# Row tiles of a selective scan: both directions' rows side by side in DRAM, the middle group's partitions interleaved, and the next tile's pieces in a new order

## The chip, the cores and the metric

The kernel runs on one core of one Trainium2 chip. The metric is the device time of one launch in microseconds (us), as the median of several runs. All engine times below come from one profiled execution of the program.

The engines are named as in the profile: PE is TensorE (matmuls; PEld its weight loads), DVE is VectorE, ACT is ScalarE, POOL is GpSimd and SP is the sync engine, which here does nothing but issue DMAs, in order, each after the semaphores that it needs.

## The reference

The input is x, of 2 images x 96 channels x 128 x 128 in fp32. The model is two blocks. The first mixes with a four-direction Mamba, the second with a 3x3 convolution, and each is followed by a small feed-forward net in emulated low precision. The change concerns the Mamba alone:

```python
x = x + L0_conv(_ln_c(x))          # norm over channels, then four scans
# L = 16384 positions; four orders: rows, rows reversed, columns, columns reversed
def _mamba(x, ...):                # D_INNER 192, D_STATE 16, DT_RANK 6, causal conv of 4 taps
    xc, z = split(x @ in_w.T)
    xc = silu(conv(xc) + conv_b)
    dt_raw, Bm, Cm = split(xc @ xproj_w.T)
    dt = softplus(dt_raw @ dt_w.T + dt_b)
    A = -exp(A_log)                # 192 x 16
    def step(h, t):                # h: 192 x 16
        h = exp(dt_t[:, :, None] * A) * h + dt_t[:, :, None] * B_t[:, None, :] * u_t[:, :, None]
        y = einsum('bds,bs->bd', h, C_t)
    y = (y + Dp * xc) * silu(z)
    return y @ outp_w.T
out = concat([y1, y2, y3, y4]) @ fuse_w.T + fuse_b
```

B_t and C_t are 16 numbers per position and direction, and every one of the 192 inner channels of that direction uses the same ones.

## The kernel before, in words

Each image (batch) passes three stages one after the other: `normalize`, `mamba`, and `ffn_and_conv`. `acc`, 96 x 16384 in SBUF, holds the running activations. `normalize` also writes the normalized input to DRAM twice, in row order (`xnr`) and in column order (`xnc`).

**Pairs, groups, tiles.** `mamba` takes the four directions as two pairs, (0, 2) forwards and (1, 3) reversed. The 2 x 192 = 384 inner channels of a pair make three groups of 128 partitions: group 0 is 128 channels of the first direction, group 2 is 128 channels of the second, and the middle group, 1, holds the last 64 of the first on partitions 0 to 63 and the first 64 of the second on 64 to 127. Time is cut into 32 tiles of T = 512 positions. So there are 64 tiles per batch (two pairs x 32), and 128 in all.

**Units.** A tile is worked through in 24 units, each one group and two of the 16 states: 8 units of group 0, 8 of group 1, 8 of group 2. The loop index k runs over all units of all tiles. For unit k:

- `decay` (L330, ACT): two exponentials give `da`, 128 x 2 x 512, in PSUM; three buffers.
- `b_part` (L324, POOL): the row tile of B times `dtu` (dt times u), in place.
- `scan` (L334, DVE): two scans of 512 positions, written over `da`.
- `behind` (one unit later): the product of `da` with the row tile of C (L409, DVE), the last column kept in `hst` (L410, ACT), and `sums` (L341, PE), which adds the two states' products into `y` by matmuls with the identity.
- At a group's first unit, `gated` (L349, DVE) multiplies the finished `y` of the previous group with the gate `sz`, and a matmul with `dmat` (L416, PE) begins a new `y`. `y` has a single PSUM bank.
- `project` and `collect` (L357 to L365) take a finished pair of groups through the output weights `gmat` into `acc`.

`decay` and `b_part` run two units ahead of the scan (`AHEAD = 2`).

**Row tiles.** B and C are wanted on all partitions, so the rows are written to DRAM once per tile and read back as broadcasts. `rows` (L251) projects xc to 64 rows (and the 12 of dt), `rows_out` (L258 to L261) copies them to SBUF and writes them to DRAM four times (`COPIES = 4`), side by side as `bcd[copy, B or C, 32 rows, T]`. A row tile (`row_tile`, L320) is 128 partitions x 4 states x 512, 1 MB: a quad of states for one group. Each partition reads 8 KB, and the partitions take the four copies in turn. For groups 0 and 2 that is one DMA. The middle group's two halves belong to different directions, so its row tile takes two DMAs of 64 partitions. `fetch` issues a B tile every other unit three quads ahead and a C tile two quads ahead; there are four buffers of B rows and three of C rows.

**The next tile's pieces.** Tile n + 1 is prepared while tile n is scanned. `prologue` lists its pieces as (step, where, function): at unit `step` of tile n, either before the scans (`where` 0) or at the end of the unit (1). All five queues are written in program order (`in_order`), so the list settles the order in each engine's queue:

```python
at = [(0, 0, load), (8, 1, partial(silu, "xc")), (14, 1, partial(silu, "sz"))]
at += [(12, 0, rows), (12, 1, rows_out)]
for g, k in enumerate((4, 5, 6)):
    at += [(k, 0, partial(conv, g)), (k, 1, partial(conv_out, g))]
for g, k in enumerate((7, 10, 11)):
    at += [(k, 0, partial(gate, g)), (k, 1, partial(gate_out, g))]
for g, k in enumerate((13, 18, 21)):
```

`conv` and `gate` are matmuls into `misc`, a single PSUM bank that all these pieces and `project` share (`inproj`, L207); `conv_out` (L233) and `gate_out` (L241) are ScalarE's copies out of it. In the middle group the two directions' matmuls write partitions 0 to 63 and 64 to 127. `silu` (L244, L245) is one activation over all three groups between two loads of an activation table. The last loop places dt's pieces per group: `dt_in` (a matmul, L268), `dt_exp` and `dt_ln` (three ScalarE operations each, L273 to L284), then four GpSimd operations (L287 to L297).

Of the kernel before, what the change touches and what calls it, by code (L numbers as in the profile page):

```python
# [10 lines left out]
F32 = mybir.dt.float32  # L11
# [3 lines left out]
AF = mybir.ActivationFunctionType  # L15
# [5 lines left out]
C = 96  # L21
W = 128
L = W * W
T = 512
NT = L // T
R = T // W
S = 16
RK = 6
DI = 192
HID = 384  # L30
PAIRS = ((0, 2), (1, 3))
NG = 3
COPIES = 4
B_AHEAD = 3
C_AHEAD = 2
AHEAD = 2
# [1 line left out]
BCO = 32  # L38
NBC = 4 * S
# [3 lines left out]
def tile_metaformer(ctx: ExitStack, tc: tile.TileContext, a: dict, out: bass.AP):  # L43
    nc = tc.nc
# [22 lines left out]
    convb = const("convb", (128, 2, NG))  # L67
    bcw = const("bcw", (128, 2, NG, BCO + NBC))
    dtw = const("dtw", (2 * RK, 2, NG * 128))
# [6 lines left out]
    dmat = cpool.tile([128, 2, NG, 128], F32, name="dmat")  # L76
    gmat = cpool.tile([128, 2, NG + 1, C], F32, name="gmat")
    inx = cpool.tile([C, 4, 4, DI], F32, name="inx")
    nc.vector.memset(gmat, 0.0)
    with tc.tile_pool(name="prep", bufs=1) as pp, tc.tile_pool(name="prep_ps", bufs=2, space=PSUM) as pps:  # L80
        alog = pp.tile([128, 2, NG, S], F32, name="alog")
        nc.sync.dma_start(alog, a["alog"])
        nc.scalar.activation(alog, alog, AF.Exp)
        nc.vector.tensor_scalar_mul(amat, alog, -1.0)

        dskip = pp.tile([128, 2, NG], F32, name="dskip")
        nc.sync.dma_start(dskip, a["dskip"])
        for pi in range(2):
            for g in range(NG):
                nc.vector.tensor_scalar_mul(dmat[:, pi, g, :], ident, dskip[:, pi, g : g + 1])  # L90

        inxw = pp.tile([C, 4, DI], F32, name="inxw")
        nc.sync.dma_start(inxw, a["inx"])
        taps = pp.tile([C, 4, 4, DI], F32, name="taps")
        nc.sync.dma_start(taps, a["taps"].broadcast_to((C, 4, 4, DI)))
        for d in range(4):
            nc.vector.tensor_tensor(inx[:, d], taps[:, d], inxw[:, d, None, :].broadcast_to((C, 4, DI)), ALU.mult)
        outw = pp.tile([C, 4, DI], F32, name="outw")
        nc.sync.dma_start(outw, a["outw"])
        fusew = pp.tile([C, 4, C], F32, name="fusew")  # L100
        nc.sync.dma_start(fusew, a["fusew"])
        for pi, (da, db) in enumerate(PAIRS):

            pieces = [
                (slice(0, 128), da, 0, 128),
                (slice(0, 64), da, 128, 192),
                (slice(64, 128), db, 0, 64),
                (slice(0, 128), db, 64, 192),
            ]
            for g, (rows, d, lo, hi) in enumerate(pieces):  # L110
                ps = pps.tile([128, C], F32, name="ps")
                nc.tensor.matmul(ps[rows, :], outw[:, d, lo:hi], fusew[:, d, :], start=True, stop=True)
                nc.vector.tensor_copy(gmat[rows, pi, g, :], ps[rows, :])

    def layernorm(x, eps, dst, wp, psp, bufs=2, **cast):

# [66 lines left out]
    def mamba(acc, xnr, xnc):  # L183

        with ExitStack() as st:
            pool = lambda n, bufs, **kw: st.enter_context(tc.tile_pool(name=n, bufs=bufs, **kw))
            io, one, two, gen = pool("io", 1), pool("one", 1), pool("two", 2), pool("gen", 4)
            ps_w, ps_y, ps_m = (pool(n, k, space=PSUM) for n, k in (("ps_w", 3), ("ps_y", 1), ("ps_m", 1)))
            rows_d = pool("rows_d", 3, space=DRAM)
# [20 lines left out]
            def prologue(pi, i, d):  # L210

                rev = pi == 1
                lo = L - (i + 1) * T if rev else i * T
                src = []
# [13 lines left out]
                    d["ps"] = inproj(pi, g, lambda dd, k, lo, hi: inx[:, dd, k, lo:hi], src, (0, 1, 2, 3))  # L228

                def conv_out(g):  # L230
                    if g == 0:
                        d["xc"] = two.tile([128, NG, T], F32, name="xc")
                    nc.scalar.activation(d["xc"][:, g, :], d["ps"], AF.Identity, bias=convb[:, pi, g : g + 1])  # L233

                def gate(g):
                    d["ps"] = inproj(pi, g, lambda dd, k, lo, hi: inz[:, dd, lo:hi], src, (3,))

                def gate_out(g):
                    if g == 0:
                        d["sz"] = two.tile([128, NG, T], F32, name="sz")  # L240
                    nc.scalar.copy(d["sz"][:, g, :], d["ps"])  # L241

                def silu(name):
                    nc.scalar.activation(d[name], d[name], AF.Silu)  # L244
# [8 lines left out]
                        )  # L253

                def rows_out():

                    d["rows"] = one.tile([BCO + NBC, T], F32, name="rows")
                    nc.scalar.copy(d["rows"], d["ps"][0 : BCO + NBC, :])  # L258
                    d["bcd"] = rows_d.tile([COPIES, 2, NBC // 2, T], F32, name="bcd")
                    for n in range(COPIES):  # L260
                        nc.sync.dma_start(d["bcd"][n].rearrange("k r t -> (k r) t"), d["rows"][BCO:, :])  # L261

# [35 lines left out]
                    d["dtu"].append(dtu)  # L298


                at = [(0, 0, load), (8, 1, partial(silu, "xc")), (14, 1, partial(silu, "sz"))]
                at += [(12, 0, rows), (12, 1, rows_out)]
                for g, k in enumerate((4, 5, 6)):
                    at += [(k, 0, partial(conv, g)), (k, 1, partial(conv_out, g))]
                for g, k in enumerate((7, 10, 11)):
                    at += [(k, 0, partial(gate, g)), (k, 1, partial(gate_out, g))]
                for g, k in enumerate((13, 18, 21)):
                    pieces = (0, 0, dt_in), (0, 1, dt_exp), (1, 1, dt_ln), (2, 0, dt_q), (3, 0, dt_log), (3, 0, dt_sum), (4, 0, dt_u)
                    at += [(k + m, where, partial(f, g)) for m, where, f in pieces]
                return sorted(at, key=lambda p: p[:2])  # L310

            def row_tile(d, g, s, k, ahead):

                t = gen.tile([128, 4, T], F32, name=f"row{k}", bufs=ahead + 1)
                for half in range(2) if g == 1 else (slice(None),):
                    rows = slice(half * 64, half * 64 + 64) if g == 1 else half
                    at = s + S * (half if g == 1 else g // 2)
                    n = (64 if g == 1 else 128) // COPIES
                    src = d["bcd"][None, :, k, at : at + 4, :].broadcast_to((n, COPIES, 4, T))
                    nc.sync.dma_start(t[rows], src)  # L320
                return t

            def b_part(d, g, b):
# [58 lines left out]
            for _, _, f in prologue(*steps[0], state[0]):  # L382
                f()
            bs, cs, das, hs = {}, {}, {}, {}

            def fetch(k, n, ahead, m):
                if k < total:
                    t = row_tile(state[k // nu], *units[k % nu], n, ahead)
                    m[k], m[k + 1] = t[:, 0:2, :], t[:, 2:4, :]
# [46 lines left out]
            for k in range(total + 6):  # L436
                n, u = divmod(k, nu)
# [128 lines left out]
def _layout(v):  # L566

    f = np.float32
    order = [d for pair in PAIRS for d in pair]
    rows = lambda w: w[order].reshape(2, NG, 128, -1).transpose(2, 0, 1, 3)  # L570
    xw = v["L0_conv_xproj_w"]
    bcw = np.zeros((2, 2 * DI, BCO + NBC), f)
    dtw = np.zeros((2 * RK, 2, 2 * DI), f)
    for pi, pair in enumerate(PAIRS):
        for k, d in enumerate(pair):
            at = slice(k * DI, (k + 1) * DI)
            for j in range(2):
                to = slice(BCO + (2 * j + k) * S, BCO + (2 * j + k + 1) * S)
                bcw[pi, at, to] = xw[d, RK + j * S : RK + (j + 1) * S].T
            bcw[pi, at, k * RK : (k + 1) * RK] = xw[d, :RK].T  # L580
            dtw[k * RK : (k + 1) * RK, pi, at] = v["L0_conv_dt_w"][d].T
    grouped = lambda w: w.reshape(2, NG, 128, -1).transpose(2, 0, 1, 3)
    out = {
        "x": v["x"].reshape(NB, C, L),
        "ident": np.eye(128, dtype=f),
        "inx": v["L0_conv_in_w"][:, :DI].transpose(2, 0, 1),
        "inz": v["L0_conv_in_w"][:, DI:].transpose(2, 0, 1),
        "taps": v["L0_conv_conv_w"].transpose(0, 2, 1)[None],
        "convb": rows(v["L0_conv_conv_b"])[..., 0],
        "bcw": grouped(bcw),  # L590
        "dtw": dtw,
        "dtb": rows(v["L0_conv_dt_b"])[..., 0],
        "alog": rows(v["L0_conv_A_log"]),
        "dskip": rows(v["L0_conv_Dp"])[..., 0],
        "outw": v["L0_conv_outp_w"].transpose(1, 0, 2),
        "fusew": v["L0_conv_fuse_w"].reshape(C, 4, C).transpose(2, 1, 0),
        "fuseb": v["L0_conv_fuse_b"].reshape(C, 1),
        "kw": v["L1_conv_kernel"].transpose(1, 2, 3, 0).reshape(C, 9, C),
    }
    for n in range(2):  # L600
        p = f"L{n}_ffn_"
        out[f"w1_{n}"] = v[p + "W1"].T
        out[f"b1_{n}"] = v[p + "b1"].reshape(3, 128).T
        out[f"w2_{n}"] = v[p + "W2"].T.reshape(3, 128, C).transpose(1, 0, 2)
        out[f"b2_{n}"] = v[p + "b2"].reshape(C, 1)
    return {k: np.ascontiguousarray(w) for k, w in out.items()}
# [16 lines left out]
```

## Time and profile before

| | before |
|---|---|
| time, median of 3 | 13002.14 us (12996.56 to 13002.71) |
| span of the profiled execution | 13002.5 us |
| first scan of batch 0, of batch 1 | 168 us, 6661 us |
| mean of a tile | 90.13 us |
| mean granted TensorE clock | 0.963 |
| DMA, whole span | 3400 MB, 262 GB/s |

The two scan stages, 128 tiles x 90.13 us, are 11,537 us of the 13,002. The time and the span are the same thing measured in two ways. A group of instructions in the profile is named by line, engine, operation and tiles (out<-in), and "<-" after a wait names the instruction whose end released it. The times inside a tile that are given below are from the tile that begins at 3138.95 us.

The DMAs that the change touches, with their size in KB and the median time from issue to landing in us:

```profile
row<-bcd SPq DMA_DIRECT2D x2048, 1024.0 KB, 7.5
row<-bcd SPq DMA_DIRECT2D x2048, 512.0 KB, 8.0
bcd<-rows SPq DMA_DIRECT2D x512, 128.0 KB, 9.8
```

### The profile page before, as it was taken

What the parts mean: (1) busy time and instruction counts of PE and PEld (TensorE: products, weight loads), DVE (VectorE), ACT (ScalarE), POOL (GpSimd) and SP (SyncE); (2) the same over time, 40 slices, a digit from 0 to 9 for tenths busy, and PEclk for the clock granted to TensorE, in tenths of its full rate; (3) what the DMA queues carried; (4) which work ended last, traced back from release to release, by engine and by line L of the source; (5) the groups of instructions that cost most, each with busy time, mean ns of one, the idle gap of its engine ahead of it and who ended that gap; (6) DMA issues with size and microseconds to landing.
All of it is one profiled execution on the core that took longest, in us unless ns stands there. A gap on an engine that the chain in (4) does not pass through costs nothing. (4 is left out here: it accounts for less than half of the span.)

```text
span 13002.5 us, 97992 instructions
## 1 busy us (share of the span) xinstructions
PE 10850.3 (83%) x24208; PEld 3987.1 (31%) x24208; DVE 11569.1 (89%) x10865; ACT 8560.0 (66%) x14738; POOL 9215.4 (71%) x4772
## 2 busy tenths in 40 slices
PE   6888888888888888888978888888888888888889
PEld 2323233333333333333323333332333333333233
DVE  5999999999999999995459999999999999999954
ACT  6666666666666666665566666666666666666655
POOL 4877778777787787772147778777787777877721
PEclk8999999999999999999989999999999999999999
DMA  7999999999999999992079999999999999999920
GB/s 226 287 294 282 298 288 285 295 283 298 288 285 295 283 295 289 285 295 68 13 226 285 298 283 292 290 285 298 285 291 291 284 298 286 290 294 281 296 61 13
DMA packets 545331, 3400.40 MB, mean 262 GB/s; under 512 B 81612, under 2 KB 82732, under 8 KB 146840
## 3 DMA queue, kind: packets, MB, share of 16 engines
q1 hardware_dynamic: 544760, 3394.12, 83.1%
q8 instruction: 195, 3.19, 0.1%
q14 instruction: 376, 3.08, 0.1%
HBM read 3288.94 MB, written 104.86 MB: 261 GB/s over the span
## 5 line engine op out<-in xcount | busy, mean ns | idle before, releaser
L324 POOL TENSOR_TENSOR row<-dtu,row 128x1024 f32<-128x1024 f32 x3072 | 7175.7, 2358 | 1739.3 <-DMA row<-bcd 1419.2
L334 DVE TENSOR_TENSOR_SCAN da<-da,hst,row 128x512 f32<-128x512 f32 x5952 | 7339.4, 1274 | 351.2 <-ACT da L330 194.6
L341 PE MATMUL y<-row,ident 128*128 128x512 f32 x12288 | 6120.1, 626 | 1113.3 <-DVE row L409 1098.9
L330 ACT ACTIVATE da<-dt,amat 128x512 f32<-128x512 f32 x6144 | 4249.4, 692 | 207.5 <-ACT hst L410 0.4
L341 PEld LDWEIGHTS y<-row,ident 128*128 128x128 f32 x12288 | 2288.9, 197 | 4779.4 <-DVE row L409 2292.3
L409 DVE TENSOR_TENSOR row<-da,row 128x1024 f32<-128x1024 f32 x3072 | 3705.9, 1206 | 19.6 <-DMA row<-bcd 18.8
L410 ACT COPY hst<-da 128x2 f32<-128x2 f32 x3072 | 484.0, 158 | 2235.5 <-DVE row L409 2233.3
L416 PE MATMUL y<-xc,dmat 128*128 128x512 f32 x768 | 526.1, 773 | 779.1 <-DVE sz L349 779.1
L287 POOL TENSOR_TENSOR q<-e,q 128x512 f32<-128x512 f32 x384 | 488.0, 1271 | 821.8 <-ACT hst L410 709.1
L233 ACT ACTIVATE xc<-misc,convb 128x512 f32<-128x512 f32 x384 | 264.2, 688 | 1117.5 <-PE misc L207 1117.5
L207 PE MATMUL misc<-xa,inx 96*128 96x512 f32 (+1 forms) x2048 | 932.4, 597 | 59.0 <-DMA xa<-xnr 57.2
L207 PE MATMUL misc<-xb,inx 96*64 96x512 f32 (+1 forms) x2048 | 928.1, 595 | 1.6 <-ACT xc L233 1.6
L531 POOL TENSOR_TENSOR acc<-acc,y 96x512 f32<-96x512 f32 x128 | 147.6, 1153 | 987.0 <-DVE y L530 987.0
L541 PE MATMUL pc<-pad,kw 96*96 96x512 f32 x1152 | 566.7, 593 | 0.0
L207 PEld LDWEIGHTS misc<-xa,inx 96*128 96x128 f32 (+1 forms) x2048 | 323.6, 163 | 625.5 <-issue 493.4
L293 POOL TENSOR_TENSOR dt<-dt,ln 128x512 f32<-128x512 f32 x384 | 486.9, 1268 | 30.1
L297 POOL TENSOR_TENSOR dtu<-dt,xc 128x512 f32<-128x512 f32 x384 | 488.5, 1272 | 0.5
L290 POOL TENSOR_TENSOR ln<-ln,q 128x512 f32<-128x512 f32 x384 | 488.1, 1271 | 0.5
L359 PE MATMUL misc<-sz,gmat 128*96 128x512 f32 x1024 | 483.6, 594 | 0.0
L416 PEld LDWEIGHTS y<-xc,dmat 128*128 128x128 f32 x768 | 129.0, 211 | 1102.1 <-DVE sz L349 1099.1
L268 PE MATMUL misc<-rows,dtw 12*128 12x512 f32 x768 | 439.7, 652 | 18.5 <-ACT dt L275 17.2
L132 DVE TENSOR_TENSOR xq<-xm,rs 96x512 fp8e5<-96x512 f32 x128 | 87.9, 687 | 387.8 <-ACT rs L128 387.8
(75 smaller groups left out, 8403.8 us busy)
## 6 DMA issues: line engine op xcount, KB each, us to landing
row<-bcd SPq DMA_DIRECT2D x2048, 1024.0 KB, 7.5
row<-bcd SPq DMA_DIRECT2D x2048, 512.0 KB, 8.0
bcd<-rows SPq DMA_DIRECT2D x512, 128.0 KB, 9.8
xa<-xnr SPq DMA_DIRECT2D x124, 193.1 KB, 5.8
xb<-xnc SPq DMA_DIRECT2D x124, 193.1 KB, 5.5
acc<-in_x_dram SPq DMA_DIRECT2D x16, 768.0 KB, 17.8
xnr<-xn SPq DMA_DIRECT2D x16, 768.0 KB, 4.3
xnc<-stg SPq DMA_DIRECT2D x16, 768.0 KB, 5.6
```

Source lines behind the costliest of these rows:

```text
L207: nc.tensor.matmul(ps[rows, :], w(PAIRS[pi][d], k, lo, hi), src[d][:, k : k + T], **se)
L287: nc.gpsimd.tensor_tensor(d["q"], d["e"], d["q"], ALU.subtract)
L290: nc.gpsimd.tensor_tensor(d["ln"], d["ln"], d["q"], ALU.add)
L293: nc.gpsimd.tensor_tensor(d["dt"][g], d["dt"][g], d["ln"], ALU.add)
L297: nc.gpsimd.tensor_tensor(dtu, d["dt"][g], d["xc"][:, g, :], ALU.mult)
L324: nc.gpsimd.tensor_tensor(b, d["dtu"][g][:, None, :].broadcast_to((128, 2, T)), b, ALU.mult)
L330: nc.scalar.activation(da[:, j, :], d["dt"][g], AF.Exp, scale=amat[:, pi, g, s + j : s + j + 1])
L334: nc.vector.tensor_tensor_scan(h[:, j, :], da[:, j, :], b[:, j, :], 0.0 if i == 0 else hst[:, g, s + j : s + j + 1], ALU.mult, ALU.add,)
L341: nc.tensor.matmul(y, ident, c[:, j, :], start=False, stop=s + j == S - 1)
L409: nc.vector.tensor_tensor(c, h, c, ALU.mult)
L416: nc.tensor.matmul(y, dmat[:, pi, g, :], d["xc"][:, g, :], start=True, stop=False)
L541: nc.tensor.matmul(pc, kw[:, t, :], rows, start=t == 0, stop=t == 8)
```

## The change

It has two parts that belong together.

**One DMA per row tile.** The rows in DRAM are laid out as [B or C, quad, direction, state in the quad, T], in one copy. The two directions' blocks of 8 KB for a quad are now neighbours. Groups 0 and 2 read one block on all partitions. The middle group has its channels reordered, so that its even partitions belong to the first direction and its odd ones to the second, and one DMA of 128 partitions reads the two blocks in turn. The small weights are permuted on the host to match. Two of the middle group's inputs, xc and sz, come out of the matmuls in halves as before; `conv_out` and `gate_out` write them to a tile of their own (`mix_xc`, `mix_sz`), and `mix` brings them into the interleaved order with two SBUF-to-SBUF DMAs each.

**A new order of the pieces.** So that those DMAs have time, the middle group's convolution and gate are made first. All gates now come after the group change at unit 8, each copy out stands half a step or a whole step after its matmul, the row projection moves behind unit 11's sums, `rows_out` is split from the DRAM write, and sz's activation moves from step 14 to 13, with dt's pieces after it.

```diff
-COPIES = 4
                 def conv_out(g):
-                    if g == 0:
+                    if g == 1:
                         d["xc"] = two.tile([128, NG, T], F32, name="xc")
-                    nc.scalar.activation(d["xc"][:, g, :], d["ps"], AF.Identity, bias=convb[:, pi, g : g + 1])
+                    t = mixed("xc") if g == 1 else d["xc"][:, g, :]
+                    nc.scalar.activation(t, d["ps"], AF.Identity, bias=convb[:, pi, g : g + 1])
...
-                    nc.scalar.copy(d["sz"][:, g, :], d["ps"])
+                    nc.scalar.copy(mixed("sz") if g == 1 else d["sz"][:, g, :], d["ps"])
+
+                def mixed(name):
+                    d["mix", name] = one.tile([128, T], F32, name=f"mix_{name}")
+                    return d["mix", name]
+
+                def mix(name):
+
+                    for k in range(2):
+                        nc.sync.dma_start(d[name][k:128:2, 1, :], d["mix", name][64 * k : 64 * k + 64, :])
...
-                    d["bcd"] = rows_d.tile([COPIES, 2, NBC // 2, T], F32, name="bcd")
-                    for n in range(COPIES):
-                        nc.sync.dma_start(d["bcd"][n].rearrange("k r t -> (k r) t"), d["rows"][BCO:, :])
+
+                def rows_to_dram():
+
+                    d["bcd"] = rows_d.tile([2, S // 4, 2, 4, T], F32, name="bcd")
+                    nc.sync.dma_start(d["bcd"].rearrange("k q d s t -> (k q d s) t"), d["rows"][BCO:, :])
...
-                at = [(0, 0, load), (8, 1, partial(silu, "xc")), (14, 1, partial(silu, "sz"))]
-                at += [(12, 0, rows), (12, 1, rows_out)]
-                for g, k in enumerate((4, 5, 6)):
-                    at += [(k, 0, partial(conv, g)), (k, 1, partial(conv_out, g))]
-                for g, k in enumerate((7, 10, 11)):
-                    at += [(k, 0, partial(gate, g)), (k, 1, partial(gate_out, g))]
-                for g, k in enumerate((13, 18, 21)):
-                    pieces = (0, 0, dt_in), (0, 1, dt_exp), (1, 1, dt_ln), (2, 0, dt_q), (3, 0, dt_log), (3, 0, dt_sum), (4, 0, dt_u)
+                at = [(0, 0, load), (8, 1, partial(silu, "xc")), (13, 1, partial(silu, "sz"))]
+                at += [(12, 1, rows), (13, 0, rows_out), (13, 1, rows_to_dram)]
+                at += [(5, 0, partial(mix, "xc")), (10, 1, partial(mix, "sz"))]
+                for g, k, where in ((1, 3, 1), (0, 5, 0), (2, 6, 1)):
+                    at += [(k, where, partial(conv, g)), (k + 1, where, partial(conv_out, g))]
+                for g, k in ((1, 9), (0, 10), (2, 11)):
+                    at += [(k, 1, partial(gate, g)), (k + 1, 0, partial(gate_out, g))]
+                for g, k in enumerate((14, 17, 20)):
+                    pieces = (0, 1, dt_in), (1, 0, dt_exp), (1, 1, dt_ln), (3, 0, dt_q), (4, 0, dt_log), (4, 0, dt_sum), (5, 0, dt_u)
...
             def row_tile(d, g, s, k, ahead):

                 t = gen.tile([128, 4, T], F32, name=f"row{k}", bufs=ahead + 1)
-                for half in range(2) if g == 1 else (slice(None),):
-                    rows = slice(half * 64, half * 64 + 64) if g == 1 else half
-                    at = s + S * (half if g == 1 else g // 2)
-                    n = (64 if g == 1 else 128) // COPIES
-                    src = d["bcd"][None, :, k, at : at + 4, :].broadcast_to((n, COPIES, 4, T))
-                    nc.sync.dma_start(t[rows], src)
+
+                src = d["bcd"][k, s // 4] if g == 1 else d["bcd"][k, s // 4, g // 2 : g // 2 + 1]
+                n = src.shape[0]
+                nc.sync.dma_start(t, src[None].broadcast_to((128 // n, n, 4, T)))
                 return t
```

Left out here: `gmat` is built from zero-padded weights with full-width matmuls in place of half-width ones and a memset, once at the start, and the host permutes the weights.

More of the change, by code (lines that the diff above doesn't have):

```diff
@@ L78, in tile_metaformer @@
     inx = cpool.tile([C, 4, 4, DI], F32, name="inx")
-    nc.vector.memset(gmat, 0.0)
     with tc.tile_pool(name="prep", bufs=1) as pp, tc.tile_pool(name="prep_ps", bufs=2, space=PSUM) as pps:
@@ L97, in tile_metaformer @@
             nc.vector.tensor_tensor(inx[:, d], taps[:, d], inxw[:, d, None, :].broadcast_to((C, 4, DI)), ALU.mult)
-        outw = pp.tile([C, 4, DI], F32, name="outw")
-        nc.sync.dma_start(outw, a["outw"])
+        outx = pp.tile([C, 2, NG + 1, 128], F32, name="outx")
+        nc.sync.dma_start(outx, a["outx"])
         fusew = pp.tile([C, 4, C], F32, name="fusew")
         nc.sync.dma_start(fusew, a["fusew"])
[L102 to L110, printed above, removed]
+        for pi, pair in enumerate(PAIRS):
+            for g in range(NG + 1):
                 ps = pps.tile([128, C], F32, name="ps")
-                nc.tensor.matmul(ps[rows, :], outw[:, d, lo:hi], fusew[:, d, :], start=True, stop=True)
-                nc.vector.tensor_copy(gmat[rows, pi, g, :], ps[rows, :])
+                nc.tensor.matmul(ps, outx[:, pi, g, :], fusew[:, pair[g // 2], :], start=True, stop=True)
+                nc.vector.tensor_copy(gmat[:, pi, g, :], ps)
     def layernorm(x, eps, dst, wp, psp, bufs=2, **cast):
@@ L238, in gate_out @@
                 def gate_out(g):
-                    if g == 0:
+                    if g == 1:
                         d["sz"] = two.tile([128, NG, T], F32, name="sz")
-                    nc.scalar.copy(d["sz"][:, g, :], d["ps"])
+                    nc.scalar.copy(mixed("sz") if g == 1 else d["sz"][:, g, :], d["ps"])
[5 more added lines that the diff above has]
+                        nc.sync.dma_start(d[name][k:128:2, 1, :], d["mix", name][64 * k : 64 * k + 64, :])
                 def silu(name):
@@ L569, in _layout @@
     order = [d for pair in PAIRS for d in pair]
-    rows = lambda w: w[order].reshape(2, NG, 128, -1).transpose(2, 0, 1, 3)
+    perm = np.arange(2 * DI)
+    perm[128:256] = perm[128:256].reshape(2, 64).T.reshape(-1)
+    grouped = lambda w: w.reshape(2, NG, 128, -1).transpose(2, 0, 1, 3)
+    plain = lambda w: grouped(w[order].reshape(2, 2 * DI, -1))
+    rows = lambda w: grouped(w[order].reshape(2, 2 * DI, -1)[:, perm])
     xw = v["L0_conv_xproj_w"]
@@ L577, in _layout @@
             for j in range(2):
-                to = slice(BCO + (2 * j + k) * S, BCO + (2 * j + k + 1) * S)
-                bcw[pi, at, to] = xw[d, RK + j * S : RK + (j + 1) * S].T
+                to = [BCO + 2 * j * S + 8 * (s // 4) + 4 * k + s % 4 for s in range(S)]
+                bcw[pi, at, to] = xw[d, RK + j * S : RK + (j + 1) * S]
             bcw[pi, at, k * RK : (k + 1) * RK] = xw[d, :RK].T
             dtw[k * RK : (k + 1) * RK, pi, at] = v["L0_conv_dt_w"][d].T
-    grouped = lambda w: w.reshape(2, NG, 128, -1).transpose(2, 0, 1, 3)
+    outx = np.zeros((C, 2, NG + 1, 128), f)
+    for pi, (p, q) in enumerate(PAIRS):
+        ow = v["L0_conv_outp_w"]
+        outx[:, pi, 0] = ow[p, :, :128]
+        outx[:, pi, 1, 0::2] = ow[p, :, 128:]
+        outx[:, pi, 2, 1::2] = ow[q, :, :64]
+        outx[:, pi, 3] = ow[q, :, 64:]
     out = {
@@ L588, in _layout @@
         "taps": v["L0_conv_conv_w"].transpose(0, 2, 1)[None],
-        "convb": rows(v["L0_conv_conv_b"])[..., 0],
-        "bcw": grouped(bcw),
-        "dtw": dtw,
+        "convb": plain(v["L0_conv_conv_b"])[..., 0],
+        "bcw": grouped(bcw[:, perm]),
+        "dtw": dtw[:, :, perm],
         "dtb": rows(v["L0_conv_dt_b"])[..., 0],
@@ L594, in _layout @@
         "dskip": rows(v["L0_conv_Dp"])[..., 0],
-        "outw": v["L0_conv_outp_w"].transpose(1, 0, 2),
+        "outx": outx,
         "fusew": v["L0_conv_fuse_w"].reshape(C, 4, C).transpose(2, 1, 0),
```

## The prediction

> **What bounds the kernel now.** I read the page's busy shares and slices first, then VectorE's list of waits, then the timeline of one tile on each engine, and last the DMA views, because the change is made in the DMA and its effect has to arrive at VectorE.
>
> ```profile
> PE 10850.3 (83%) x24208; PEld 3987.1 (31%) x24208; DVE 11569.1 (89%) x10865; ACT 8560.0 (66%) x14738; POOL 9215.4 (71%) x4772
> DVE  5999999999999999995459999999999999999954
> DMA  7999999999999999992079999999999999999920
> ```
>
> DVE and DMA both stand at 9 in the scan stage, so the page alone doesn't say which one limits. VectorE's waits do:
>
> ```profile
> DVE da L334 <- ACT da L330: 199.4, 126, 1.9
> DVE da L334 <- POOL row L324: 171.9, 8, 84.4
> DVE sz L349 <- PE y L341: 171.0, 128, 2.1
> DVE da L334 <- ACT hst L410: 139.4, 123, 1.6
> DVE da L334 <- issue: 21.2, 51, 0.8
> DVE row L409 <- DMA row<-bcd: 18.8, 28, 2.1
> ```
>
> The columns are the total in us, the number of times and the longest. There are 128 tiles (64 per batch), so three of these waits happen once per tile. The 171.9 is two waits of 84.4 at the two starts of the scan stage, and hardly anything is a DMA. All three per-tile waits can be seen in one tile:
>
> ```profile
> 3165.55 1.21 DVE L409 TENSOR_TENSOR row<-da,row 128x1024 f32<-128x1024 f32 x1
> 3170.26 1.28 DVE L334 TENSOR_TENSOR_SCAN da<-da,hst,row 128x512 f32<-128x512 f32 x1
> 3173.29 1.29 DVE L334 TENSOR_TENSOR_SCAN da<-da,hst,row 128x512 f32<-128x512 f32 x1 [1.75 <-ACT da L330]
> 3177.02 0.69 DVE L349 TENSOR_TENSOR sz<-y,sz 128x512 f32<-128x512 f32 x1 [1.32 <-PE y L341]
> ...
> 3204.58 1.29 DVE L334 TENSOR_TENSOR_SCAN da<-da,hst,row 128x512 f32<-128x512 f32 x1 [1.27 <-ACT hst L410]
> ```
>
> Elsewhere VectorE runs without a gap: two products in a row start at 3003.80 and 3007.28, so a unit (two states of one group) takes 3.49 us. A tile is 24 units and three gatings of 0.59, or 24 x 3.488 + 1.8 = 85.5 us. Tiles take 89.9 us, and the difference is the waits: 366 us (2.9 per tile) around unit 9, and 139 us (1.1 per tile) at unit 17. The bound is VectorE plus some 4.3 us per tile in which ScalarE and TensorE make it wait while they prepare the next tile.
>
> Why the first two happen is seen on the other two engines:
>
> ```profile
> 3165.66 0.69 ACT L233 ACTIVATE xc<-misc,convb 128x512 f32<-128x512 f32 x1 [3.13 <-PE misc L207]
> 3171.00 0.69 ACT L233 ACTIVATE xc<-misc,convb 128x512 f32<-128x512 f32 x1 [3.15 <-PE misc L207]
> ...
> 3167.37 3.60 PE L207 MATMUL misc<-xb,inx 96*128 96x512 f32 x8
> 3172.52 1.02 PE L207 MATMUL misc<-xa,inz 96*128 96x512 f32 x2
> 3173.38 3.60 PE L341 MATMUL y<-row,ident 128*128 128x512 f32 x8
> ```
>
> ScalarE stands 3.1 us at each copy out of the convolution, with the next decay queued behind it. TensorE has no gap from 3145.47 to 3176.98: the three convolutions, the projection and the first gate push the sums back until the gating at 3177.02 has to wait for them. A matmul record costs 0.4285 us (start to start), a convolution is 8 of them (3.43 us), a unit's sums 4 (1.71 us), a gate 2 (0.86 us).
>
> The DMA side, by stretch (the last two columns are the busy share of the DMA engines and GB/s):
>
> ```profile
> 3163.00:3195.00 32.00, 30.32 (x76) 10.96 (x72) 28.93 (x26) 21.22 (x36) 19.42 (x10) 1.00 0.95 229
> 3198.50:3216.00 17.50, 12.33 (x23) 4.68 (x24) 16.23 (x16) 13.14 (x23) 12.86 (x8) 0.90 0.93 384
> 8.00:11.50 3.50, 0.00 (x0) 0.00 (x0) 1.38 (x7) 0.28 (x1) 0.00 (x0) 1.00 0.98 227
> ```
>
> In the first stretch mostly the middle group's half loads run, at 229 GB/s; in the second whole loads, at 384 GB/s. By the trace's packet records an 8192-byte packet takes about 620 ns in the first and 312 ns in the second. The third is the load of `taps`, one DRAM row sent to 96 partitions, and I come back to it.
>
> [...] after the idle 2.10 us before unit 0's first product the records come 0.853 us apart until 3149.4, so TensorE begins each tile's preparation late. The change doesn't touch that gap.
>
> **The change, part by part.**
>
> *Whole loads for the middle group.* Sixteen issues of 512 KB per tile become eight of 1 MB. Per engine a tile's row loads are now 16 DMAs x 8 packets x 0.312 us plus 8 x 8 x 0.62, some 80 us; after, 24 x 8 x 0.312 = 60 us. This removes most of POOL's 1419 us of waiting for rows, but POOL is ahead of VectorE, so of it only the 18.8 us at L409 and some 3 us of the small waits on POOL reach the end: 22 us.
>
> *One DRAM copy in place of four.* Three writes of 128 KB per tile go; they were hidden. All 128 partitions (64 in the middle group) now read one 8 KB block. Bounds: 312 ns per packet if that is harmless; if it behaves as `taps` did (about 870 ns for 12288 bytes), 580 ns per 8 KB. I take 312. In a whole load the packet records show the engines' n-th packets all starting within about 0.15 us of each other, and partitions take the copies in turn, so I infer that all 16 engines already read the same copy at the same time, at full speed. And the loads of `x`, whose rows are all different, also came at 225 GB/s (16 to 28 us), so the rate of `taps` need not come from its one row.
>
> *Mixing DMAs.* Four SBUF-to-SBUF DMAs of 128 KB per tile are new. On SP, xc's wait for ScalarE's copy of the middle convolution (ready near 3161.2 on the example tile's clock); queued behind them are row loads whose buffers are not free before then anyway (xc's own turn comes only when unit 3's sums, at about 3162.0, free a row tile). Landing in the usual 8 us, they are there at about 3170; the activation at step 8 wants them near 3174.8. No cost, 4 us in hand.
>
> *The order of the pieces.* The copies out now come half a step or a step after their matmuls, so ScalarE's 3 us waits shrink. Walking the in-order queues: decay 8 is ready at about 3167.9 and wanted at 3167.9, decay 9 at 3169.5 and wanted at 3171.4; the 1.75 us wait for decay goes. But the gating still needs TensorE's sums, and TensorE's stretch loses only the first gate (now at step 10): 31.5 - 0.86 = 30.7 us, so y is ready near 3176.1. Without any wait VectorE would gate at 3177.02 - 1.32 - 1.75 = 3173.95. It still waits 2.2 us where it lost 3.07. So one wait takes the place of the other, and the gain is 0.87 per tile.
>
> *The later wait (unit 17).* Now ScalarE does sz's activation with its two table loads (4.05 us) and dt_ln (1.96 us) between two decays. In the new order dt_ln follows a later decay, but the row projection stands behind unit 11's sums, so `rows_out` waits: in times of the same tile, projection done near 3191.6, `rows_out` 3192.25, decay 15 at 3193.85, activation to 3197.9, decay 16 at 3199.5, wanted at 3198.65. That leaves 0.9 us at unit 16 for 1.13 at unit 17: 0.2 gained.
>
> *At no price:* gmat's build and dropped memset (once, in preparation); permuted weights; the first tile's mixing (two landings of a few us against three fewer DMA issues per batch).
>
> Sum: 126 x (0.87 + 0.23) + 22 = 161 us, so 13002 - 161 = 12841 us.
>
> **The rivals.**
> 1. *The order was the whole trouble:* both waits vanish, which saves 366 + 139 + 22 = 527 us, hence 12475, or with half of the remainder staying about 12560. For it: all waits sit in the moved pieces. Against: TensorE's unbroken 31 us.
> 2. *Hidden anyway:* TensorE pays the saved 0.86 back in new handovers of the single `misc` bank (each convolution now waits for ScalarE's copy half a step later). About 12990.
> 3. *The mixing is late (slower):* the longest row landing is 16.4 us. A landing at 3179 puts the activation 4.2 us back; 0.75 is in hand, so 3.4 per tile, 126 x 3.4 = 430, less 161: 13270. Against: the queue in front is shorter at 312 ns per packet.
> 4. *One source is slow (slower):* 24 x 8 x 0.58 = 111 us and some 4 for small packets, 115 per tile. Outside the tiles lie 13002 - 128 x 90.13 = 1466 us, so about 16190. [...] the lockstep above speaks against.
>
> **How the numbers follow.** Forecast 0.64, rival 1 0.08, rival 2 0.08, rival 3 0.08, rival 4 0.12. Faster is the forecast and rival 1: 0.72. Same is rival 2: 0.08. Slower are 3 and 4: 0.20. The range leaves out rival 4 and about half of rival 1, and reaches up to rival 3: 12560 to 13280.
>
> **What would show it.** Right: 8192-byte packets near 312 ns in all stages and the DMA slices down from 9 to about 7; POOL's wait for rows a fraction of 1419 us; VectorE's wait for ACT da near nothing and for PE y grown from 171 to about 270 us; about 110 us left of ACT at unit 16. Wrong: DMA digits still at 9 with POOL or L409 waiting for rows (rival 4), the activation of xc waiting for a DMA (rival 3), or PE y also gone (rival 1).

## The result and the profile after

The changed kernel takes 12900.92 us (median of 4 runs, 12894.32 to 12905.01) against 13002.32 us for the kernel before (the 13002.14 above, with a fourth run), a ratio of 0.9923 [0.9905, 0.994]. It is faster by 101 us where 161 was forecast. The profiled execution spans 12903.2 us (13002.5 before), and the mean tile is 89.35 us (90.13).

First the page of the changed kernel: VectorE's and the DMA's busy slices, and the DMA issues with their count, size and median time to landing.

```profile
DVE  5999999999999999995459999999999999999954
DMA  6777777777777777771067777777777777777710
row<-bcd SPq DMA_DIRECT2D x3072, 1024.0 KB, 5.0
xc<-mix_xc SPq DMA_DIRECT2D x256, 128.0 KB, 5.4
sz<-mix_sz SPq DMA_DIRECT2D x256, 128.0 KB, 5.5
bcd<-rows SPq DMA_DIRECT2D x128, 128.0 KB, 2.2
```

The DMA part did what it was built for. The slices fall from 9 to 7, every row tile is one DMA of 1 MB, and it lands in 5.0 us where it took 7.5 or 8.0. By the trace's packet records a tile's 8 KB packets, which are the row loads, take 66.2 us on each of the 16 DMA engines (79.7 before).

Now VectorE's waits in the changed kernel (total us, times, longest). Lines have moved: L336 is the scan (L334 before), L351 the gating (L349), L411 the product (L409), L343 the sums (L341).

```profile
DVE sz L351 <- PE y L343: 269.2, 137, 2.3
DVE da L336 <- POOL row L326: 185.0, 27, 85.0
DVE da L336 <- issue: 139.5, 154, 1.4
DVE da L336 <- POOL dtu L300: 43.2, 45, 1.6
```

The wait for ACT da (199.4 before) is gone, the one for PE y has grown from 171.0 to 269.2, and L409's wait for a DMA is gone. Two lines have to be read with care. "issue" says that the profile saw nothing that was waited for, and dtu had been finished before its wait ended. In both cases the last thing to end was a decay on ScalarE, as the timelines below show. Sorting VectorE's idle time by unit of the tile gives the balance, in us over the whole program:

| VectorE's time at | before | forecast | after |
|---|---|---|---|
| unit 9 (decay 9 and the gating) | 366.3 | 256 | 262.7 |
| unit 17 before; units 16 and 17 after | 139.6 | 111 | 124.8 |
| waits for row tiles (L409 and small ones at L334) | 20.5 | 0 | 0 |
| unit 8 | 23.6 | 23.6 | 30.6 |
| unit 20 | 0 | 0 | 45.4 |
| VectorE busy | 11569.1 | 11569.1 | 11555.8 |

The differences add up to -99.8 us, and the spans differ by 99.3.

**Unit 9.** TensorE in one tile of the changed kernel (it begins at 2127.30 us; start, duration, engine, line):

```profile
2137.30 1.98 PE L343 MATMUL y<-row,ident 128*128 128x512 f32 x4 [0.65 <-DVE row L411]
...
2149.77 3.60 PE L199 MATMUL misc<-xa,inx 96*128 96x512 f32 x8
2153.21 3.60 PE L343 MATMUL y<-row,ident 128*128 128x512 f32 x8
2156.64 3.60 PE L199 MATMUL misc<-xb,inx 96*128 96x512 f32 x8
2160.08 3.60 PE L343 MATMUL y<-row,ident 128*128 128x512 f32 x8
2164.46 1.13 PE L418 MATMUL y<-xc,dmat 128*128 128x512 f32 x2 [0.78 <-DVE sz L351]
```

Between 2137.30 and 2163.68 TensorE has no gap. The projection of the previous tile, three convolutions and the sums fill it, and only then can VectorE gate. On VectorE this is the first line here:

```profile
2163.72 0.69 DVE L351 TENSOR_TENSOR sz<-y,sz 128x512 f32<-128x512 f32 x1 [2.07 <-PE y L343]
...
2187.47 1.29 DVE L336 TENSOR_TENSOR_SCAN da<-da,hst,row 128x512 f32<-128x512 f32 x1 [0.95 <-issue]
...
2203.02 1.29 DVE L336 TENSOR_TENSOR_SCAN da<-da,hst,row 128x512 f32<-128x512 f32 x1 [0.89 <-POOL dtu L300]
```

It waits 2.07 us; the two waits here were 1.75 and 1.32 before. The second line is unit 16, the third unit 20. ScalarE's timeline of the same tile shows what unit 16 waits for:

```profile
2179.52 0.58 ACT L259 COPY rows<-misc 96x512 f32<-96x512 f32 x1 [3.01 <-PE misc L253]
...
2181.63 1.28 ACT L246 ACT_TABLE_LOAD   x1
2182.92 1.48 ACT L246 ACTIVATE sz<-sz 128x1536 f32<-128x1536 f32 x1
2184.42 1.28 ACT L247 ACT_TABLE_LOAD   x1
2185.72 0.16 ACT L412 COPY hst<-da 128x2 f32<-128x2 f32 x1
2185.97 1.42 ACT L332 ACTIVATE da<-dt,amat 128x512 f32<-128x512 f32 x2
```

`rows_out` waits 3.01 us for the row projection, sz's activation with its two table loads follows, and decay 16 ends at 2187.39; the scan starts 0.08 us later.

**Unit 20, which the forecast did not have.** The wait comes in 47 of the 128 tiles. In the new order `dt_in` of group 1 stands directly behind the group change on TensorE (step 17), and `dt_exp` in front of decay 20 on ScalarE (step 18). TensorE at that point in two tiles of the changed kernel, the first with the wait, the second without:

```profile
585.61 2.08 PE L418 MATMUL y<-xc,dmat 128*128 128x512 f32 x2 [1.57 <-DVE sz L351]
587.48 2.98 PE L343 MATMUL y<-row,ident 128*128 128x512 f32 x4
590.39 1.12 PE L271 MATMUL misc<-rows,dtw 12*128 12x512 f32 x2
...
1927.94 1.13 PE L418 MATMUL y<-xc,dmat 128*128 128x512 f32 x2 [0.78 <-DVE sz L351]
1928.90 1.88 PE L343 MATMUL y<-row,ident 128*128 128x512 f32 x4
1930.71 1.12 PE L271 MATMUL misc<-rows,dtw 12*128 12x512 f32 x2
```

The same matmuls reach `dt_in` 4.78 us after the group's start in the first tile and 2.77 us in the second: the first starts at half clock (0.85 us per record in place of 0.43). ScalarE waits for it, with decay 20 behind. In the first tile decay 20 is the second line here, and VectorE's scan follows its end at once; the last line is the tile without the wait:

```profile
591.61 0.69 ACT L276 ACTIVATE e<-misc,dtb 128x512 f32<-128x512 f32 x1 [4.43 <-PE misc L271]
...
593.47 1.42 ACT L332 ACTIVATE da<-dt,amat 128x512 f32<-128x512 f32 x2
...
594.98 1.29 DVE L336 TENSOR_TENSOR_SCAN da<-da,hst,row 128x512 f32<-128x512 f32 x1 [1.25 <-issue]
...
1931.93 0.69 ACT L276 ACTIVATE e<-misc,dtb 128x512 f32<-128x512 f32 x1 [2.47 <-PE misc L271]
```

The trace also records the clock that TensorE was granted. It is at half from 582.85 to 589.68 us in the first tile, and from 1924.29 to 1927.70 in the second, where it ends just before group 2 begins. Over the 128 tiles this separates without exception: in the 47 with the wait, half clock covers at least 0.77 us of group 2's first 2 us, in the other 81 none of them.

When the clock falls can be read from the same records. All its changes lie on one grid with a step of 3.413 us. While batch 0 is scanned (170 to 6400 us), 78 steps at full clock were followed by half clock, and TensorE was busy, by its matmul records, for 0.84 to 1.74 us in them. In the 1650 that were followed by full clock it was busy for 1.47 us or more. Ahead of group 2 TensorE waits for VectorE again and again (2.84 and 1.57 us in the first tile), so in which tiles half clock reaches group 2 seems to depend on where the grid falls. This is read from the traces; no run was made to test it.

**The DMA queue behind it.** GpSimd's wait for rows (the first fence, changed kernel) was to fall to a fraction of 1419 us; it is 1051.9. SP's own waits (the second fence, same kernel; the two lines were 4676.5 and 1552.5 before) point to why: a row load is issued when its buffer comes free, and these waits did not shrink in sum (6229.0 before, 6887.4 now) while the landing went from 7.5 or 8.0 us to 5.0.

```profile
POOL q L290 <- ACT hst L412: 1071.2, 172, 9.1
POOL row L326 <- DMA row<-bcd: 1051.9, 406, 5.8
```

```profile
SPq L322 <- PE y L343: 4617.8, 1530, 6.5
SPq L322 <- DVE row L411: 2269.6, 1281, 5.1
```

### The profile page after: what moved, and what is told of

Same layout as the page of the kernel before. It is cut to its first block, busy times and chain, and to the rows that moved or that the text cites. A ratio compares the mean times of both kernels' runs of the same rounds, so it can differ in the third digit from the quotient of the medians.

```text
span 12903.2 us, 96320 instructions
## 1 busy us (share of the span) xinstructions
PE 10779.3 (84%) x24208; PEld 3972.8 (31%) x24208; DVE 11555.8 (90%) x10864; ACT 8524.6 (66%) x14738; POOL 9215.0 (71%) x4772
## 5 line engine op out<-in xcount | busy, mean ns | idle before, releaser
L326 POOL TENSOR_TENSOR row<-dtu,row 128x1024 f32<-128x1024 f32 x3072 | 7176.3, 2356 | 1282.3 <-DMA row<-bcd 1051.9
L336 DVE TENSOR_TENSOR_SCAN da<-da,hst,row 128x512 f32<-128x512 f32 x5952 | 7317.5, 1269 | 188.4 <-issue 133.1
L343 PE MATMUL y<-row,ident 128*128 128x512 f32 x12288 | 6135.6, 628 | 1366.1 <-DVE row L411 1365.6
L343 PEld LDWEIGHTS y<-row,ident 128*128 128x128 f32 x12288 | 2261.7, 195 | 5031.0 <-DVE row L411 2741.1
L411 DVE TENSOR_TENSOR row<-da,row 128x1024 f32<-128x1024 f32 x3072 | 3692.5, 1202 | 0.1
L199 PE MATMUL misc<-xa,inx 96*64 96x512 f32 (+1 forms) x2048 | 932.1, 597 | 58.9 <-DMA xa<-xnr 57.1
L418 PE MATMUL y<-xc,dmat 128*128 128x512 f32 x768 | 471.5, 698 | 537.9 <-DVE sz L351 537.9
L226 ACT ACTIVATE xc<-misc,convb 128x512 f32<-128x512 f32 x256 | 176.0, 687 | 807.4 <-PE misc L199 807.4
L276 ACT ACTIVATE e<-misc,dtb 128x512 f32<-128x512 f32 x384 | 261.5, 681 | 460.3 <-PE misc L271 448.5
L199 PEld LDWEIGHTS misc<-xa,inx 96*64 96x64 f32 (+1 forms) x2048 | 323.3, 163 | 622.8 <-issue 523.1
L351 DVE TENSOR_TENSOR sz<-y,sz 128x512 f32<-128x512 f32 x384 | 261.6, 681 | 269.8 <-PE y L343 269.2
```

The lines of the kernel that those rows point to most:

```text
L199: nc.tensor.matmul(ps[rows, :], w(PAIRS[pi][d], k, lo, hi), src[d][:, k : k + T], **se)
L326: nc.gpsimd.tensor_tensor(b, d["dtu"][g][:, None, :].broadcast_to((128, 2, T)), b, ALU.mult)
L336: nc.vector.tensor_tensor_scan(h[:, j, :], da[:, j, :], b[:, j, :], 0.0 if i == 0 else hst[:, g, s + j : s + j + 1], ALU.mult, ALU.add,)
L343: nc.tensor.matmul(y, ident, c[:, j, :], start=False, stop=s + j == S - 1)
L411: nc.vector.tensor_tensor(c, h, c, ALU.mult)
```

## The experiments

All ratios are to the kernel before, timed on the same chip (13002.24, 13000.88 and 13001.53 us in the three sets), with the 95% interval. The expectations name two theories of the gain: that the order of the pieces brings it (A), with the gating held by TensorE's stretch, or that something else does, the row loads above all.

**e1_order: the new order alone, on the old DRAM layout.** The list `at` of the changed kernel without its two `mix` lines and `rows_to_dram`; four copies, half loads, no interleaving.

```diff
-                at += [(12, 1, rows), (13, 0, rows_out), (13, 1, rows_to_dram)]
+                at += [(12, 1, rows), (13, 0, rows_out)]
-                at += [(5, 0, partial(mix, "xc")), (10, 1, partial(mix, "sz"))]
```

> The new order of the pieces alone, on the old layout: four DRAM copies, two half loads per middle row tile, no mixing. Theory A (the order brought the gain, because the first gate left TensorE's stretch before the gating): about 12,905 to 12,930 us, VectorE waits about 260 us for PE y and none for the decay behind the convolution; DMA digits stay at 9. Theory B (the relief of the DMA brought it): about 13,000 us. In both, if A and B share, something like 12,950.

Measured: 12917.44 us, 0.9936 [0.9919, 0.9952]. VectorE's waits in this kernel:

```profile
DVE sz L349 <- PE y L341: 273.3, 149, 2.3
...
DVE da L334 <- issue: 105.1, 128, 1.7
```

85 of the 101 us come from the order. The exchange of ACT da for PE y is there without any new DMA, and so is the wait at unit 20 (41.6 us). The DMA slices stay at 9 and L409 still waits 14.5 us for rows. The changed kernel is 16.5 us faster than this one; the runs of the two do not overlap (12913.27 to 12919.93 and 12894.32 to 12905.01), though the intervals of their ratios do.

**e2_layout: the new layout with the old order.** The list `at` of the kernel before, with the mixing put where its inputs are ready.

```diff
+                at += [(12, 0, rows), (12, 1, rows_out), (12, 1, rows_to_dram)]
+                at += [(6, 0, partial(mix, "xc")), (11, 0, partial(mix, "sz"))]
```

> The new layout alone (one copy, whole loads, mixing) with the old order of convolutions, gates, rows and dt. Theory A: 12,975 to 13,000 us, the two waits at unit 9 as before (some 199 for the decay and 167 for PE y), only the 19 us for rows at L409 gone; DMA digits at 7. Theory B: about 12,900 us.

Measured: 12995.79 us, 0.9995 [0.9987, 1.0004]: no change that can be told from none. VectorE's waits in this kernel:

```profile
DVE da L336 <- ACT da L332: 194.6, 123, 1.9
...
DVE sz L351 <- PE y L343: 170.6, 128, 2.1
DVE da L336 <- ACT hst L412: 161.1, 126, 1.6
```

The first two are as before the change. The third was 139.4: it has grown by about as much as L409's wait, now gone, had taken.

**e3_copies: the changed kernel with four copies in DRAM again.** Groups 0 and 2 read the four in turn, the middle group the first one.

```diff
-                    d["bcd"] = rows_d.tile([2, S // 4, 2, 4, T], F32, name="bcd")
+                    d["bcd"] = rows_d.tile([4, 2, S // 4, 2, 4, T], F32, name="bcd")
...
+                    src = d["bcd"][None, :, k, s // 4, g // 2].broadcast_to((32, 4, 4, T))
```

> The changed kernel with four DRAM copies again for groups 0 and 2 (the middle group reads the first copy). Theory: one 8 KB block read by all partitions costs nothing, so 12,900 us within 0.2%, 8192-byte packets at 312 ns as in the changed kernel, median landing near 5.0 us. Rival: the copies spread the reads and rows land earlier, POOL waits less than 1052 us for rows; time lower only if that reaches VectorE.

Measured: 12900.49 us, 0.9922 [0.9908, 0.9937], the changed kernel's time. An 8192-byte packet takes 350 ns on average, against 345 with one copy, and a row tile lands in 5.4 us in the median, against 5.0. Reading one block on 128 partitions costs nothing here. GpSimd's wait for rows, which the rival saw falling, is 1074.7 us against 1051.9.

**e8_copyout: the kernel before, with the convolutions' copies out half a step later.** This tests the forecast's account of the wait for decay.

```diff
-                    at += [(k, 0, partial(conv, g)), (k, 1, partial(conv_out, g))]
+                    at += [(k, 0, partial(conv, g)), (k + 1, 0, partial(conv_out, g))]
```

> The kernel before with one edit: each convolution's copy out stands half a step later (at the start of the next unit), gates and all else as before. Theory A (TensorE's stretch sets the gating): the wait for the decay (199 us) goes and PE y grows from 167 to about 370, time 12,990 to 13,005 us, the same. Rival C (the late copies out bring the gain): PE y stays near 167 and the time falls to about 12,800 to 12,850.

Measured: 12999.92 us, 0.9999 [0.999, 1.0007]. The time is theory A's, but the exchange that it foresaw did not take place. VectorE's waits in this kernel:

```profile
DVE da L334 <- ACT da L330: 199.1, 126, 1.9
DVE sz L349 <- PE y L341: 171.4, 129, 2.1
```

Half a step is too little, since the last copy out, now at step 7, still stands between decays 8 and 9 in ScalarE's queue. So this run could not set theory A against rival C; e7, without late copies, does.

**e7_gate0: the kernel before, with only the first gate moved behind the gating.**

```diff
-                for g, k in enumerate((7, 10, 11)):
+                for g, k in enumerate((9, 10, 11)):
```

> The kernel before with one edit: the first gate moves from step 7 to step 9, behind the gating of unit 8. Theory A (TensorE's unbroken stretch before the gating is the size of the loss): 0.86 us per tile less, PE y falls from 167 to about 60 us in 126 waits while the decay's 199 stays, time about 12,890 to 12,900. Rival D (the gain of the change needed the convolutions' new order): no more than 20 us faster.

Measured: 12918.86 us, 0.9934 [0.9919, 0.9949]. VectorE's waits in this kernel:

```profile
DVE da L334 <- ACT hst L410: 284.6, 219, 1.9
...
DVE row L409 <- DMA row<-bcd: 95.9, 117, 3.0
...
DVE sz L349 <- PE y L341: 63.0, 130, 2.1
```

One line of the list brings 82 of the 101 us; the time expected was some 20 us lower. The wait for y falls from 171.0 to 63.0 and the one for decay 9 stays (196.6 us, now under ACT hst). Unit 9 as a whole comes to 254.6 us, and to 262.7 in the changed kernel, where the wait for decay 9 is gone (262.9 in e1): its going alone brings nothing as long as the stretch on TensorE is there. Unit 17 falls from 139.6 to 89.4. L409's wait for a row grows from 18.8 to 95.9. The half loads alone don't explain that: e1 has them too, is as early at unit 9, and waits 14.5 us. Why the rows come later here was not found.

**e4_project: the changed kernel, with group 2's projection moved past the gating too.** It stood at step 3 of the next tile; the loop's end moves with it.

```diff
-                    later(k + 4, 0, project, pi, i, d, g)
-                    later(k + 4, 1, collect, pi, d, g)
+                    later(k + (4 if g == 1 else 10), 0, project, pi, i, d, g)
+                    later(k + (4 if g == 1 else 10), 1, collect, pi, d, g)
```

> The changed kernel with group 2's projection moved from step 3 to step 9 of the next tile, so that its 3.4 us of matmuls leave TensorE's stretch before the gating. Theory A: the wait for y at unit 9 (263 us) goes to under 30, time about 12,630 to 12,660. Rival E (something else, ScalarE's copies or the rows of C, holds VectorE there as well): a wait of another kind takes its place at units 8 to 11, time 12,750 to 12,900.

Measured: 12818.65 us, 0.9859 [0.9842, 0.9875]; the expectation was missed by some 160 us. VectorE's waits in this kernel:

```profile
DVE da L336 <- issue: 225.1, 261, 1.8
...
DVE sz L351 <- PE y L343: 58.8, 131, 2.1
```

Unit 9 fell from 262.7 to 53.8 us, where under 30 was expected, and unit 8's 30.6 went as well. The 3.4 us of matmuls taken out bring forward the gating by 1.66 us only: TensorE now catches up with VectorE and waits for it once more, at unit 3, so the stretch without a gap begins 13.5 us into the tile in place of 10.0, and its 21.3 us (26.4 in the changed kernel) still end 0.4 us after VectorE is ready. But unit 16 rose from 122.0 to 170.9, unit 20 from 45.4 to 92.2 (84 tiles now start group 2 at half clock), and unit 12 is new with 44.7: 140 us of the 240 given back, by VectorE's idle time (the kernel's time fell by 82). So the stretch does set the gating, and the three later waits take up much of what is gained ahead of them.

**e5_silu: the changed kernel, with sz's activation and dt's pieces moved.** The activation and group 0's pieces are one step later, groups 1 and 2 have `dt_in` and `dt_exp` half a step and the rest a step later, so that `dt_exp` of group 1 follows decay 20.

```diff
+                at = [(0, 0, load), (8, 1, partial(silu, "xc")), (14, 1, partial(silu, "sz"))]
...
+                for g, k in enumerate((15, 17, 20)):
...
+                    if g > 0:
+                        pieces = ((1, 0, dt_in), (1, 1, dt_exp), (2, 1, dt_ln), (4, 0, dt_q), (5, 0, dt_log), (5, 0, dt_sum), (6, 0, dt_u))
```

> The changed kernel with sz's activation one step later (14) and dt's pieces spread: group 0 one step later, groups 1 and 2 with their matmul half a step later. Theory F (unit 16 waits because rows_out, itself waiting for TensorE's row projection, and the activation stand between two decays; unit 20 waits because group 1's dt matmul stands right behind the group change on TensorE): both waits (122 and 45 us) go, time about 12,730 to 12,760. Rival: they move to units 17 to 21 under another name, time within 30 us of 12,900.

Measured: 12735.32 us, 0.9795 [0.978, 0.981], as expected. VectorE's waits in this kernel:

```profile
DVE sz L353 <- PE y L345: 268.9, 128, 2.3
...
DVE da L338 <- issue: 48.9, 81, 1.4
```

Units 16 and 20 no longer wait; what is left under "issue" is unit 8. The wait for y is untouched. The run moves all of this at once, so it doesn't say what each move is worth.

**e6_both and e6_again: the edits of e4 and e5 together.**

> The two edits of e4_project and e5_silu together. If the waits are independent, the gains add up: about 12,460 to 12,500 us, VectorE without a wait worth naming in the tiles, a tile near 85.6 us. If TensorE or POOL has no room left at that pace, 12,550 to 12,700 with a new wait.

> e6_both once more, on the same chip as e9_best_old_layout, for the comparison: 12,524 us within 0.2%.

Measured: 12523.61 us, 0.9632 [0.9618, 0.9647], and in another set 12524.31, 0.9632 [0.9616, 0.9649]. That is 477 us faster than the kernel before and 377 faster than the changed one, and 24 slower than the expected range. VectorE's waits in e6_both:

```profile
DVE sz L353 <- PE y L345: 58.0, 128, 2.1
DVE da L338 <- issue: 44.7, 124, 0.7
```

From e5 to here these two lines fall by 215 us and the time by 212. What e4 had given back at units 16 and 20 is not given back once these units have room. Left are 53.8 us at unit 9 and 44.7 at unit 12. In one tile of e6_both (2105 us) ScalarE waits 1.58 us for the matmuls of the first gate, with decay 12 behind its copy; decay 12 ends at 2107.20, and the scan starts 0.08 us later.

**e9_best_old_layout: the order of e6 on the old DRAM layout.** Four copies, half loads and the old inputs, no mixing; all other pieces stand as in e6.

> The order of e6_both on the old layout (four copies, half loads, no mixing): what is the layout worth at the faster pace? Theory G (the half loads need some 84 us of DMA time per tile, too close to a tile of 86.3): rows come late, waits for row<-bcd appear at L409 or behind POOL, 12,600 to 12,750 us. Rival H (the DMA still hides): 12,510 to 12,540 us, as e6_both.

Measured: 12555.46 us, 0.9659 [0.9645, 0.9674], 31 us slower than e6 and between what the two theories expected. The DMA slices of this kernel, and then those of e6_both:

```profile
DMA  7999999999999999991079999999999999999910
```

```profile
DMA  6888888888888888881068888888888888888810
```

At this pace all DMA packets of a tile take 83.4 us per engine of a tile of 86.6 with the old layout, and 70.1 of 86.3 with the new one (e6_again). The old layout's packets fill 96% of the tile, the new one's 81%. The two profiled executions differ by 36.0 us. L411 waits 27.6 us for rows, and VectorE is busy for 7.5 us more; that accounts for nearly all of it.

## Why the prediction was right, and where it was wrong

The forecast of "faster" held, for the reason given; the sum was 161 where 101 came.

*One wait takes the place of the other at unit 9: right.* Forecast 110 us, found 104; the gating waits 2.07 us on the tile shown, where 2.2 was worked out. e7 shows that the gate leaving TensorE's stretch is what pays, and e1 that the order does it without the layout. The reason given for the end of the wait for decay was wrong: ScalarE's waits at the copies out did not shrink (1117.5 us over the 384 before, 1137.8 after). The wait went because the last copy now stands behind decay 9 in the queue; e8, where it does not, keeps it. The stretch of 31.5 us, too, is that of a tile that begins at half clock. Not each tile does, as the prediction has it, but 58 of the 128 before, and in most others the stretch is 27.3 us. After the change the two lengths are 30.7 and 26.4, so the difference of one gate is the same either way.

*Rival 1, that all waits vanish: wrong for this change, and right as a goal.* The argument against it was TensorE's stretch. e4 took more out of it and y's wait fell to 58.8 us.

*The wait at unit 16: the term was mis-sized.* The forecast was 0.9 us left per tile; it is 0.97, and unit 17 keeps 2.8 us in all. Of 29 us forecast, 15 came.

*The step that failed: the sum had no term for a wait caused by dt's pieces.* They were followed up to decay 16 and no further, though `dt_in` and `dt_exp` of group 1 had moved too, in front of decay 20. That costs 45.4 us, the largest error in the sum. e5, which moves these pieces behind decay 20, removes it. The prediction had half clock only at the start of a tile, with the remark that the change doesn't touch that gap. The same half clock at the start of group 2 decides in which tiles unit 20 waits: in the 47 that wait it covers at least 0.77 us of the group's first 2 us, in the other 81 none of them. The idle time just ahead does not decide alone: in the changed kernel's tile from 2127.30 us TensorE was idle for 2.10 us before the first product, as in the prediction's tile, and its clock was full.

*Row loads: right in size, and small as said.* 22 us were forecast. e2 found 6, which can't be told from none; at the old order unit 17 waits 21.5 us longer. Between e1 and the changed kernel it is 16.5. Packets took 309 ns in the median, 312 forecast. In the half loads they took about 620 ns (kernel before, 3163 to 3195 us), so the packets did gain by whole loads; the time followed only where somebody waited for rows.

*"A fraction of 1419 us" of GpSimd's waiting: wrong.* It is 0.74 of it. SP's waits for free buffers suggest why, and no run tested that alone. It had no weight, since GpSimd is ahead.

*Rivals 3 and 4 are out.* The mixing lands in 5.4 to 5.5 us, and no activation waits for it; e3 shows that one copy costs nothing (345 ns per packet, 350 with four). Rival 2 is out as well: the saved 0.86 us is not paid back, since 104 of the 110 us came at unit 9. How rival 1's 12560, the lower end of the range, follows was not shown; half of the 366 us between rival 1 and the forecast would give 12658.

The remaining two terms are unit 8 (+7 us; the prediction had its decay ready just when it was wanted, and the wait comes almost only in tiles that begin at half clock, 53 before and 49 of 51 after) and VectorE's busy time (-13 us). For the latter scans and products each take 4 to 5 ns less; why is open.

## What to carry to other kernels

Where one engine hands over to another at a fixed point of the loop, add up what its in-order queue holds ahead of that point: work moved past it pays (0.86 us of matmuls per tile gave 82 us) until the engine runs idle ahead of the point (e4: 3.4 us moved, 1.66 gained), and work that stays on the near side is only waited for under another name (unit 9: 262.7 us without the wait for decay 9, 254.6 in e7 with it). After moving a piece, follow every piece that moved with it to the next thing wanted behind it; a repaired wait brings the following ones forward (e4: 140 of 240 us given back), so try the repairs together before judging one. Faster transfers paid only where somebody waited for them: the same layout was worth 6 us, not told from none, at 13,002 us and 31 us at 12,524.

## What the runs showed of the hardware

- TensorE's granted clock changed only on a grid of 3.413 us steps. It went to half after steps with 0.84 to 1.74 us of recorded work, and stayed full after steps with 1.47 us or more (changed kernel, batch 0; before: up to 1.46, and 1.40 or more). The longest idle times just before it fell were 2.84 and 2.57 us in the two tiles shown at unit 20. Half clock or not moved a following matmul by 2.0 us between these two tiles of one execution.
- A block of 8 KB in DRAM read by all 128 partitions went as fast as four copies of it: 345 and 350 ns per packet on average.
- DMAs from SBUF to SBUF into every other partition, 64 partitions of 2 KB each, landed in 5.4 us (xc) and 5.5 us (sz) in the median beside the row loads (changed kernel; 3.7 and 8.4 in e2).
